# One list of instructions per engine in place of one list for TensorE and a greedy rule for the rest, with new planner constants

## The chip, the cores and the metric

The kernel runs on one core of one Trainium2 chip. The core has five engines that each work through their own stream of instructions in order and meet at semaphores: TensorE (PE, matrix products), VectorE (DVE), ScalarE (ACT, function tables), GpSimd (POOL) and SyncE (SP, which here issues nearly all DMAs). The metric is device time in microseconds for one execution. The median of three runs before the change is 3925.85 us (3921.62 to 3927.92).

## What is computed

The reference is a small vision tower: patches to tokens, one attention layer whose keys go through a Fourier series, and a mixture-of-experts network. There are 16 images of 3 x 512 x 512, which give 1024 tokens of width 256 each. Cut to what matters:

```
h = patches(x) @ W.T + b                      # 1024 tokens, 768 -> 256, per image
z = layernorm(h);  q, k, v = split(z @ w_qkv) # 8 heads of 32
k = sum_f a_f * sin(f*k) + b_f * cos(f*k)     # f = 1..256, elementwise
h = h + softmax(q k^T / sqrt(32)) v @ w_out + b_out
z = layernorm(h)
shared = relu(relu(z@sW1+sb1)@sW2+sb2)@sW3+sb3
experts = 4 networks 256 -> 128 -> 64 -> 256
h = h + shared + sum over the 2 best experts of softmax weight * expert
```

## The kernel before, in words

All times lie in `plain_path`; a second path, `general_path`, is only entered when a verdict computed on the chip asks for it.

The work on one image falls into two kinds. The first is a fixed repeating stream:

- The keys of a pair of heads are turned into angles (`keys`), written to DRAM and read back spread over partitions. `load_waves` (SP, two DMAs per tile) brings two tiles `w` per group; `load_source` and `spread_waves` (DVE shuffle) make a third, `f`. `turn_waves` (POOL) multiplies each with a lane number, `sine` (ACT) takes the sine. One group is thus three POOL and three ACT instructions.
- `mix` (M, PE, in 64x32 tiles of the array) forms partial sums of the series, `times_fast` (DVE) multiplies them, `add_up` (R, PE, 128x32 tiles) adds two groups up. 32 groups make one image, 8 groups one pair of heads. Then `finish_keys` (DVE) rounds the pair's keys and writes them to DRAM, and `stack_keys` (SP) reads them back, stacked, into the one buffer `k4`, for which the last score of the pair before must be done.
- `score` (S, PE, whole array), `exponential` (ACT, the Exp table) and `weigh` (W, PE, 128x32 tiles) are the attention: 8 key blocks for each of 8 (pair, half) attentions of an image; `normalize` (DVE) divides.

S and M write to the same pool `big` of two PSUM buffers, so the third taker has to wait until the first has been read (by the exponential, or by the product). ScalarE needs a table load (`ACT_TABLE_LOAD`) whenever it goes from sines to exponentials or back. `load_waves(g)` may only overwrite the tile that `mix(g - 4)` has read. SP issues in order, so a load that waits for its mix holds back what is queued behind it.

The second kind is everything else: tokens, layer norms, queries, values, projection, gates and networks. It is written as Python generators in four chains, 0 to 3; each `yield` names the engine of the next step. Steps of the kind "either" run with the whole array or as four 128x32 tiles, whichever tiling TensorE already has (`tiling_of`).

Nothing is scheduled at run time. While the program is built, a planner keeps a clock for each engine and places instructions one after the other; the streams that come out are fixed. In the kernel before, TensorE's order is a written string, `ORDER` (M, R, S, W or the number of a chain, 3840 tokens, of which 240 repeat 11 times). `lay_fixed` (L437) and `run` (L452) place its tokens. For SP, POOL, ACT and DVE, `others` (L408) takes whatever can start first by the planner's clock. Each step has a cost in the planner (the number in `yield ACT, 0.6` or `put(ACT, "fixed", 0.99, ...)`), and there are global constants: `LAG` between engines, `LANDS` for a DMA's landing, `SWITCH` for a change of tiling, `TABLE` for a table load.

Of the kernel before, what the change touches and what calls it, by code (L numbers as in the profile page):

```python
# [23 lines left out]
NT = N // P  # L24
# [33 lines left out]
LAG, LANDS, TABLE, PER_COLUMN = 0.06, 2.0, 1.28, 1.0 / 600  # L58
SWITCH = {None: 0.21, (128, 32): 0.13, (64, 32): 0.13}

TILINGS = {"mix": (64, 32), "av": (128, 32), "red": (128, 32)}
USERS = {"M": "prod", "S": "exp"}
KINDS = {"M": "mix", "R": "red", "S": "score", "W": "av"}
COLUMNS = (128, 32)
ORDER = (
    "333333313133100003000030M0M000MMR3R3M3M",
    "303RMM3MR330M3R3M03MSSRSSWSSWSSWWWW0MWM",
    "WMMRSSSRSWSSWSSW0WWWWMMW3MMRSSRSSWSSWSSW0WW0MMWWWMMRSSRSSWSSWSSW0WWMWWMWMRMSSSWSSWSSWSRW"
    "WWWWMMMMRSSSWSSWSSWSRWWWWW0M0MM0RMS0SSWSSWSWSWSWWW3W3MR13M3MMRSSRSSWSS1SSWWWW3WMWWM3RMS1"
    "SS1SS0SSWWWMS3WR3WWWWM0MMRMS0SS1SR1SSWW1S1SW0W1WW1MMW1W1MM1SSRWSS0SS1WSSWW10RWMWWW1MM10M"  # L70
    "S1SSRWSWR1SS1WSS1W1MMWWMMWW0SS1R1SS1WW1SS1SSW1WRW1WMMW3WMMRS1SS1SW1SS3SSW1WR1WWWWWMM13MM"
    "1RSS0SS0SS0SWWWSWWWR3MMW1WS10S1RSS1S3MMWSS3WRWWSW1WWMW31MM0SS1SSRMS1SSWWWSWR3WWWW3MM131M"
    "S1RSSWWMWSSR3S1S3S1WWW01M1WW1MM0RSS1SWSSWMS1SSWRWW01MW1WWMM101SSRMW1SSWWSS1RSS101MMWWWWW"
    "MS3SSWRMWSS1S01SSW1RW0W3MMWWRWSS131SS1MMWWSS1SSRWWW1WWW101",
    (
        "MM10RMM1SS01SS1SS1WWSS1WWWRWWWMM10MMRS3S1SS1SSWWWSS3RWWWW1W3MM0RMM3SSRSWWWSS1SS1S3WWWMMW"
        "3W311MSRM1WS1S3SWWS3S1SSRW1W0WMM1WWRMM10SS1SS1WW1SS0SSWWRW1WWW0MM10MM1SS1RRWWSS0S1SWSS1W"
        "WWWWMM1S0SRWSSWMMWS1S31SSWRW3WW1WMM3MMR1SS1SS1SSWWWSS1WRWW1WW101"
    )
    * 11,  # L80
    "MM1MM1SSRRWWS1S0SS0SSWWW130MMWW1WRM1MS1",
    "3SSRWWWSS31SS1SW1WWWWMM3RM1S0SSWSS1SSWWMSWR3WWM3WWMM13S1SR1MSWWRS3S1SWS3SWWW01MM1WW10MMR"
    "1SS1SSRWSS1S1WWS0WWWWWMM101MM1SS1RS1SRSSWWWSS01WWMMWWWMS1SSWSSRW0SS1S1WMWWR1WWMM10W1MMR1"
    "SS1SSWWSS1SSWWWR1WM1WW101MM10S1MR1SSWRS1SWSSWS1WWMMWWWRMM1SS0SSWWSSWSSRWWW1WW1M0M1RSS1SS"
    "WSSWSMWSM1WWRWM1W1WMM1RM1SS1SSWWSS1SSWR1W1W1W1MM1WWR1SM1SS1SSWWSSWS1MWWRWMWWM1SS1SWSMSRM"
    "WS1SS1WR1WWW1WW1MM1M1RSS1SWWSS1SSWSWMWW1RW1MM1RW1MM1SSR1SSWWSS1WWSSWWWW1SSSWSSWWSSWSSWWW"
    "W1SS1SS1SWWSSWWWWWW11110110111110000101000100101001000100",
)

@with_exitstack  # L90
def plain_path(ctx: ExitStack, tc: tile.TileContext, a: dict, out: bass.AP, verdict: bass.AP):
# [179 lines left out]
    def retile(tiling):  # L271

        same = now["tiling"] == tiling
        now["tiling"] = tiling
        return 0.0 if same else SWITCH[tiling]

# [53 lines left out]
    def step(c):  # L330
# [9 lines left out]
        if on:  # L340
            at = max(clock[on], ch["ready"] + LAG)
            if on == PE:
                at = max(at, banks(c)[0][0] + LAG)
            ch["ready"] = clock[on] = at + (need[1] or 0.0)
            if bank is not None:
                free[bank] = ch["ready"]
        elif isinstance(need, tuple):
            ch["ready"] = max(ch["ready"], done[need])
# [11 lines left out]
        if on == PE:  # L360
            took = PER_COLUMN * (now["stream"] - before) + retile(now["piece"])
            now["piece"] = None
            ch["ready"] = clock[PE] = at + took
# [16 lines left out]
    def wanting(engine):  # L380

        for c, ch in enumerate(chains):
            need = ch["need"]
            if ch["gen"] is None or callable(need) or need[0] != engine:
                continue
            if engine == ACT and len(need) > 2 and now["table"] != need[2]:
                continue
            at = max(clock[engine], ch["ready"] + LAG)
            if engine == PE:
                if not banks(c):  # L390
                    continue
                at = max(at, banks(c)[0][0] + LAG)
            yield at, c

    def lay(engine, queue):
        cost, deps, key, action = queues[engine][queue].pop(0)
        at = begin(engine, deps)
        clock[engine] = at + cost
        done[key] = clock[engine]
        action()  # L400

    def heads(engine):
        for rank, (name, steps) in enumerate(queues[engine].items()):
            at = begin(engine, steps[0][1]) if steps else None
            if at is not None:
                yield at, rank, name

    def others(limit):  # L408

        soonest = None  # L410
        again = True
        while again:
            again = False
            soonest = None
            for engine in (SP, POOL, ACT, DVE):
                while True:
                    settle()
                    best = min(heads(engine), default=None)
                    chain = min(wanting(engine), default=None)
                    if chain and (  # L420
                        best is None
                        or chain[0] < best[0]
                        or (chain[0] == best[0] and best[2] not in ("prod", "keys"))
                    ):
                        at, lay_it = chain[0], lambda c=chain[1]: step(c)
                    elif best:
                        at, lay_it = best[0], lambda q=best[2]: lay(engine, q)
                    else:
                        break
                    if at > limit:  # L430
                        soonest = at if soonest is None else min(at, soonest)
                        break
                    lay_it()
                    again = True
        return soonest

    def lay_fixed(kind):  # L437

        cost, deps, key, action = queues[PE][kind][0]
        user = USERS.get(kind)  # L440
        at = begin(PE, deps + (bigs[-2:-1] if user else []))

        def lay_it():
            queues[PE][kind].pop(0)
            clock[PE] = done[key] = at + cost + retile(TILINGS.get(KINDS[kind]))
            if user:
                bigs.append((user, *key[1:]))
            action()

        return at, lay_it  # L450

    def run():  # L452

        order = "".join(ORDER)
        for i, token in enumerate(order):
            now["ahead"] = order[i + 1 : i + 4]
            while True:
                soonest = others(clock[PE])
                if token in KINDS:
                    at, lay_it = lay_fixed(token)  # L460
                else:
                    c = int(token)
                    at = next((at for at, one in wanting(PE) if one == c), None)
                    lay_it = lambda: step(c)
                if at is not None and (soonest is None or at <= max(soonest, clock[PE])):
                    break
                assert soonest is not None
                others(soonest)
            lay_it()
        while (soonest := others(clock[PE])) is not None:  # L470
            others(soonest)
        assert not any(q for e in queues.values() for q in e.values())
        assert not any(ch["gen"] for ch in chains)
# [4 lines left out]
    def load_x(b, j):  # L478

        b, j = b + j // (N // XT), j % (N // XT)  # L480
        if b < B:
# [5 lines left out]
            done["x", b, j] = transfer(1.75, 0.6, clock[PE])  # L487
# [38 lines left out]
    def tokens(b, half):  # L526
# [5 lines left out]
        for t in range(4):  # L532
# [14 lines left out]
            yield DVE, 0.41  # L547
# [95 lines left out]
    def values(b):  # L643
# [5 lines left out]
        for t0 in range(0, NT, 2):  # L649
# [11 lines left out]
            yield ACT, 0.62  # L661
# [142 lines left out]
    def networks(b, half, late=False):  # L804
# [25 lines left out]
        def first_of_expert(e):  # L830
            yield ANY
            ps = hidden(lambda c: w1e[:, 2 * e + c, :], "e1p")
            yield ACT, 0.6
# [4 lines left out]
        def second_of_experts(u, e1):  # L838
# [11 lines left out]
            yield ACT, 0.6  # L850
# [15 lines left out]
        for m in range(2):  # L866
            yield ANY
            ps = hidden(lambda c, m=m: w1s[:, c, ts(m, P)], "s1p")
            yield ACT, 0.6
# [14 lines left out]
        yield ACT, 0.6  # L884
# [57 lines left out]
    def load_waves(g, j):  # L942
# [13 lines left out]
        put(SP, "waves", 1.1, deps, ("load", g, j), action)  # L956
# [29 lines left out]
    def spread_waves(g):  # L986
# [11 lines left out]
        put(DVE, "spread", 1.28, deps, ("spread", g), action)  # L998

    def turn_waves(g, j):  # L1000
# [8 lines left out]
        put(POOL, "turn", 1.87, [dep], ("turn", g, j), action)  # L1009

    def sine(g, j, change):
        def action():
            now["table"] = AF.Sin
# [6 lines left out]
        put(ACT, "fixed", 0.96 + change, [("turn", g, j)], ("sine", g, j), action)  # L1020
# [26 lines left out]
    def times_fast(g):  # L1047
# [4 lines left out]
        put(DVE, "prod", 1.16, [("mix", g), ("sine", g, 2)], ("prod", g), action)  # L1052
# [76 lines left out]
    def score(att, kc):  # L1129
# [13 lines left out]
        put(PE, "S", 0.47, deps, ("score", att, kc), action)  # L1143

    def exponential(att, kc):
        def action():
            now["table"] = AF.Exp
# [7 lines left out]
        put(ACT, "fixed", 0.99, deps, ("exp", att, kc), action)  # L1155
# [28 lines left out]
    def normalize(att):  # L1184
# [8 lines left out]
        def divide(half):  # L1193
# [11 lines left out]
            put(DVE, "norm", 0.4, deps, ("divide", att, half), action)  # L1205
# [15 lines left out]
        put(DVE, "norm", 1.67, [("av", att, NT - 1)], ("reciprocal", att), reciprocal)  # L1221
        for half in range(2):
            divide(half)
        put(DVE, "norm", 0.4, [("divide", att, 1)], ("norm", att), check)
# [45 lines left out]
    for rd in range(B * RI + 2):  # L1270
# [3 lines left out]
        for g in groups[::2]:  # L1274
            first = g == groups[0]
            for i, j in ((0, 0), (0, 1), (1, 0), (1, 1), (0, 2), (1, 2)):
                sine(g + i, j, TABLE if first and i == j == 0 else 0.0)
# [761 lines left out]
```

## Time and profile before

| | us |
|---|---|
| median of the runs | 3925.85 |
| the profiled execution, its own time | 3924.07 |
| its span, first to last instruction | 3922.5 |
| TensorE busy in the span | 3810.0 (97%) |
| ScalarE busy | 3263.0 (83%) |
| GpSimd busy | 3193.6 (81%) |
| VectorE busy | 2531.7 (65%) |
| mean granted TensorE clock | 0.994 |

The time of the profiled execution is the span and 1.6 us around it. Lines are read as: line of the kernel, engine, operation, tile written and tiles read, number of instructions, then busy time, mean duration and the idle time of the engine just before them with what ended it. Ends of matrix products are modelled in the profile and they overlap, so a TensorE that is shown as busy may be waiting inside a record: the distance between the ends of successive products tells more than the busy time. The sixteen images follow one another every 235 to 239 us in the middle of the run.

### The profile page before, as it was taken

To read this page: it belongs to the slowest core of one execution; us is meant where nothing else is said; L and a number is where in the kernel's file an instruction comes from. 1 tells how busy PE (TensorE), PEld (TensorE's weight loads), DVE (VectorE), ACT (ScalarE), POOL (GpSimd) and SP (SyncE) were. 2 spreads that over 40 slices of the span, in tenths; PEclk is the share of its full clock that TensorE was granted. 3 is DMA by queue.
4 is the path that set the end of the run, shared out by engine and by line. 5 is a ranking of instruction groups with operands and counts; after the bars stand their busy time and mean duration, and the time that the engine had idled before them with its cause. 6 is when DMAs were issued, how large, how long until landed. Compare 5 with 4: busy or idle time off the path is not lost.

```text
span 3922.5 us, 102737 instructions
## 1 busy us (share of the span) xinstructions
PE 3810.0 (97%) x40337; PEld 1948.9 (50%) x40337; DVE 2531.7 (65%) x4075; ACT 3263.0 (83%) x3939; POOL 3193.6 (81%) x2328
## 2 busy tenths in 40 slices
PE   7899999999999999999999999999999999999998
PEld 4334454554545555455454545545455454544444
DVE  4656757667675766757667675776767767576652
ACT  2788888888888888888888888888888888888983
POOL 3998878788788878879788788878879888888860
PEclk9999999999999999999999999999999999999999
DMA  7987968888787888979889788798878889788860
GB/s 228 281 261 217 278 192 245 259 226 258 220 257 225 237 264 224 259 216 256 235 233 265 212 257 247 224 265 224 262 218 255 247 229 265 216 245 235 221 170 18
DMA packets 587615, 916.51 MB, mean 234 GB/s; under 512 B 58828, under 2 KB 177524, under 8 KB 587124
## 3 DMA queue, kind: packets, MB, share of 16 engines
q1 hardware_dynamic: 580880, 906.98, 80.6%
q8 instruction: 321, 5.26, 0.6%
q10 hardware_dynamic: 6244, 2.88, 0.3%
q14 instruction: 170, 1.39, 0.1%
HBM read 758.64 MB, written 150.99 MB: 232 GB/s over the span
## 4 chain that ended last, share of the span: by engine, by line
PE 66%; DMA 13%; ACT 8%; POOL 5%; DVE 4%; issue 3%; SPq 2%; ACTq 0%; POOLq 0%; DVEq 0%
PE av L1167 17%; PE sT L1134 10%; PE kan L1036 8%; DMA w<-ud 7%; PE red L1069 4%; PE e1p L301 3%; PE tok L301 3%; ACT w L1016 3%; POOL w L1006 3%; PE e3p L301 2%; PE tok L304 2%; DMA k<-kd 2%; PE s1p L301 2%; PE e1p L304 2%; ACT f L1016 2%
## 5 line engine op out<-in xcount | busy, mean ns | idle before, releaser
L1006 POOL TENSOR_TENSOR w<-w,lane 128x1024 int32<-128x1024 int32 x1024 | 1923.6, 1895 | 406.9 <-DMA w<-ud 275.7
L1149 ACT ACTIVATE es<-sT 128x1024 f32<-128x1024 f32 x1024 | 1014.3, 1022 | 357.3 <-PE sT L1134 312.2
L1016 ACT ACTIVATE w<-w 128x1024 f32<-128x1024 int32 x1024 | 1013.4, 1046 | 67.5 <-POOL w L1006 64.3
L1006 POOL TENSOR_TENSOR f<-f,lane 128x1024 int32<-128x1024 int32 x512 | 970.2, 1895 | 102.0 <-DVE f L991 84.8
L1134 PE MATMUL sT<-q,k 128*128 128x512 f32 x2048 | 707.6, 454 | 42.9 <-DMA k<-kd 13.4
L1050 DVE TENSOR_TENSOR f<-kan,f 128x1024 f32<-128x1024 f32 x512 | 605.2, 1214 | 203.1 <-ACT f L1016 116.3
L991 DVE STREAM_SHUFFLE f<-src 128x1024 int32<-128x1024 int32 x512 | 681.3, 1370 | 0.4
L1167 PE MATMUL av<-es,v 128*32 128x256 f32 x8192 | 638.8, 383 | 3.5 <-DVE rc L1208 2.6
L1167 PE MATMUL av<-es,ones 128*32 128x256 f32 x8192 | 630.9, 379 | 0.0
L1036 PE MATMUL kan<-w,coef 64*32 64x512 f32 x8192 | 540.1, 598 | 18.8 <-ACT w L1016 12.6
L1016 ACT ACTIVATE f<-f 128x1024 f32<-128x1024 int32 x512 | 519.0, 1046 | 4.1 <-POOL f L1006 4.1
L1134 PEld LDWEIGHTS sT<-q,k 128*128 128x128 f32 x2048 | 351.2, 190 | 340.0 <-issue 146.0
L1167 PEld LDWEIGHTS av<-es,v 128*32 128x32 f32 x8192 | 235.5, 109 | 343.2 <-issue 236.9
L1167 PEld LDWEIGHTS av<-es,ones 128*32 128x32 f32 x8192 | 267.2, 110 | 176.4 <-issue 1.4
L1191 DVE RECIPROCAL rc<-av 128x256 f32<-128x256 f32 x128 | 224.8, 1756 | 169.5 <-PE av L1167 169.5
L1036 PEld LDWEIGHTS kan<-w,coef 64*32 64x32 f32 x8192 | 129.1, 105 | 313.9 <-issue 133.4
L1069 PE MATMUL red<-f,pack 128*32 128x512 f32 x2048 | 271.0, 602 | 0.0
L301 PE MATMUL tok<-wt,x 128*128 128x256 f32 x768 | 182.1, 389 | 22.1 <-DMA w1s<-in_sW 12.5
L1016 ACT ACT_TABLE_LOAD x128 | 164.2, 1283 | 17.7 <-DMA w<-ud 15.5
L304 PE MATMUL tok<-wt,x 128*32 128x256 f32 x3072 | 178.0, 380 | 0.6 <-DVE h L548 0.6
L301 PEld LDWEIGHTS tok<-wt,x 128*128 128x128 f32 x768 | 147.4, 194 | 57.9 <-DMA w1s<-in_sW 12.4
L513 ACT ACTIVATE hn<-h,less,rstd 128x256 f32<-128x256 f32 x256 | 140.7, 591 | 39.8 <-POOL less L505 39.0
(148 smaller groups left out, 4269.5 us busy)
## 6 DMA issues: line engine op xcount, KB each, us to landing
w<-ud SPq DMA_DIRECT2D x2048, 256.0 KB
q<-qd SPq DMA_DIRECT2D x512, 128.0 KB
k<-kd SPq DMA_DIRECT2D x128, 512.0 KB
x<-in_xT SPq DMA_DIRECT2D x128, 384.0 KB
ud<-u SPq DMA_DIRECT2D x64, 512.0 KB
ud<-ui SPq DMA_DIRECT2D x64, 512.0 KB
src<-ud SPq DMA_DIRECT2D x512, 64.0 KB
qd<-qhi SPq DMA_DIRECT2D x64, 256.0 KB
```

The lines of the kernel that those rows point to most:

```text
L301: nc.tensor.matmul(out=out, lhsT=lhsT, rhs=rhs, start=start, stop=stop)
L304: nc.tensor.matmul(out=out[ts(i, 32)], lhsT=lhsT[:, ts(i, 32)], rhs=rhs, start=start, stop=stop)
L991: nc.vector.stream_shuffle(w, sources[g // 8].rearrange("p r n -> p (r n)"), [4 * (g % 8) + i // 8 for i in range(32)],)
L1006: nc.gpsimd.tensor_tensor(w, w, f.to_broadcast([P, N]), ALU.mult)
L1016: nc.scalar.activation(x, w, AF.Sin, scale=TURN * 2.0**-32)
L1036: nc.tensor.matmul(out=ps[ds(64 * j + 32 * blk, 32), ts(r, 512)], lhsT=coef[ts(r, 64)].rearrange("p e f j -> p (e f j)"), rhs=w[ts(r, 64), ...
L1050: nc.vector.tensor_mul(w, kan.pop(g), w)
L1069: nc.tensor.matmul(out=rows_of_pair[p][ts(2 * i + r, 32), :], lhsT=pack[:, ds(PACK0 - 16 * (k % 2) - 2 * (k // 2), 32)], rhs=prod[:, ts(r, ...
L1134: nc.tensor.matmul(out=ps[:, ts(s, 512)], lhsT=k4[:, 2 * s + kc // 4, ts(kc % 4, P)], rhs=q4[:, s, :], start=True, stop=True,)
L1149: nc.scalar.activation(es, scores.pop(kc), AF.Exp, scale=SCALE)
L1167: nc.tensor.matmul(out=acc[0][ts(i, HD), ts(half, 256)], lhsT=ones32 if half else v[:, kc, p % NPAIR, ts(i % 2, HD)], rhs=es[:, ds(512 * ( ...
L1191: nc.vector.reciprocal(rc[0], acc[0][:, 256:512])
```

## The change

The written order of TensorE is replaced by five lists, `ORDERS`, one for each engine, each in the planner's tokens (s, e, t for sine, exponential and table step on ACT; u, p, k, n, d for DVE's queues; o for POOL; c, w, k, q for SP's; digits are the chains). TensorE's list has 3840 tokens again, of which 240 now repeat 9 times. `others`, `heads` and `wanting` go; `head` looks at the first token of each engine's list, and `run` places the token that can start first:

```diff
-    def run():
-        order = "".join(ORDER)
-        for i, token in enumerate(order):
-            now["ahead"] = order[i + 1 : i + 4]
-            while True:
-                soonest = others(clock[PE])
...
+    def run():
+        settle()
+        while any(orders.values()):
+            ready = {e: h for e in orders if (h := head(e))}
+            engine = min(ready, key=lambda e: ready[e][0])
+            token = orders[engine].pop(0)
+            now["ahead"] = orders[PE][:3]
+            ready[engine][1]()
+            settle()
...
+    def head(engine):
+        if not orders[engine]:
+            return None
+        token = orders[engine][0]
+        if token.isdigit():
+            at = wanted(engine, int(token))
+            return at is not None and (at, lambda: step(int(token)))
+        queue = token if engine == PE else TOKENS[engine][token]
+        cost, deps, key, action = queues[engine][queue][0]
+        if engine == PE:
+            at = begin(PE, deps + (bigs[-2:-1] if user_of(token, key) else []))
+            return at is not None and (at, lambda: lay_fixed(token, at))
+        at = begin(engine, deps)
+        return at is not None and (at, lambda: lay(engine, queue, at))
```

The constants of the planner change as well, and it now charges a table load wherever the kind of function changes, and a tail after each instruction before another engine may use the result:

```diff
-LAG, LANDS, TABLE, PER_COLUMN = 0.06, 2.0, 1.28, 1.0 / 600
-SWITCH = {None: 0.21, (128, 32): 0.13, (64, 32): 0.13}
+LAG, LANDS, TABLE, PER_COLUMN, STALL = 0.07, 2.3, 1.29, 1.0 / 600, 0.15
+TAIL = {"pe": 0.27, "act": 0.08, "dve": 0.06, "pool": 0.0, "sp": 0.0}
+SWITCH = {None: 0.15, (128, 32): 0.12, (64, 32): 0.12}
...
-        put(SP, "waves", 1.1, deps, ("load", g, j), action)
+        put(SP, "waves", 1.38, deps, ("load", g, j), action)
...
-        put(POOL, "turn", 1.87, [dep], ("turn", g, j), action)
+        put(POOL, "turn", 1.853, [dep], ("turn", g, j), action)
...
-        put(ACT, "fixed", 0.96 + change, [("turn", g, j)], ("sine", g, j), action)
+        put(ACT, "sine", 0.946, [("turn", g, j)], ("sine", g, j), action)
...
-        put(ACT, "fixed", 0.99, deps, ("exp", att, kc), action)
+        put(ACT, "exp", 0.91, deps, ("exp", att, kc), action)
```

No operand, tile, pool or dependency of an instruction is changed, and the matrix products, vector operations and DMAs are the same in kind and number, apart from "either" steps that now run in another tiling and apart from table loads. The letter u and the branch for "sum" in `user_of` are never reached: no queue of that name is filled.

## The prediction

> **What bounds the kernel now.** I read the page first, then busy times by stretch, then TensorE's records one by one.
>
> ```profile
> PE 3810.0 (97%) x40337; PEld 1948.9 (50%) x40337; DVE 2531.7 (65%) x4075; ACT 3263.0 (83%) x3939; POOL 3193.6 (81%) x2328
> ```
> ```profile
> 0.00:80.00 80.00, 52.90 (x186) 36.34 (x187) 33.32 (x69) 11.17 (x16) 21.34 (x40) 0.94 0.70 219
> 80.00:280.00 200.00, 177.00 (x1824) 69.70 (x1824) 123.96 (x182) 160.39 (x180) 186.16 (x110) 0.97 0.93 271
> 280.00:985.00 705.00, 689.88 (x7563) 347.32 (x7562) 470.10 (x745) 604.23 (x727) 593.91 (x420) 1.00 0.83 239
> 985.00:3349.00 2364.00, 2340.79 (x25196) 1223.92 (x25188) 1580.14 (x2542) 2035.49 (x2461) 1994.14 (x1440) 1.00 0.85 241
> 3349.00:3800.00 451.00, 442.82 (x4829) 212.72 (x4825) 289.61 (x456) 401.45 (x487) 386.71 (x285) 1.00 0.80 226
> 3800.00:3923.00 123.00, 106.65 (x763) 58.87 (x753) 34.53 (x85) 50.28 (x72) 11.38 (x36) 0.95 0.11 32
> ```
>
> The columns are the stretch, its length, then busy time (and records) of PE, weight loads, DVE, ACT and POOL, the granted clock, DMA's share and GB/s. TensorE bounds the run; only from 80 to 280 us does POOL (186 of 200 us) set the pace. But "busy" hides two things, which the timeline shows:
>
> ```profile
> 1502.68 0.40 PE L301 MATMUL wb<-w,sel 128*128 128x512 f32 x1
> 1503.01 0.64 PE L1167 MATMUL av<-es,v 128*32 128x256 f32 x8
> ...
> 1510.49 1.06 PE L1036 MATMUL kan<-w,coef 64*32 64x512 f32 x12
> 1511.49 0.70 PE L301 MATMUL e3p<-w3s,s 128*128 128x256 f32 x2
> ...
> 1514.42 1.89 PE L301 MATMUL v<-wv,hnT 128*128 128x256 f32 x8
> 1516.24 1.09 PE L1036 MATMUL kan<-w,coef 64*32 64x512 f32 x16
> ```
>
> Each line is start, duration, shapes. In one tiling, a 256-column step ends 0.216 us after the one before, a 512-column step 0.429 (0.234 for scores), a transpose 0.109. When the tiling changes, the first end comes later: v ends at 1516.31, the second of two kan steps at 1517.33, so the first at 1516.90, 0.59 after v in place of 0.429. In the same way the first e3p ends 0.42 after the last kan, and the first av 0.35 after wb, both in place of 0.216. The medians over the trace are 0.161 into 64*32, 0.138 into 128*32 and 0.194 to 0.197 into 128*128. The second hidden thing is waiting for a free PSUM buffer or for data:
>
> ```profile
> 1296.54 0.73 PE L1134 MATMUL sT<-q,k 128*128 128x512 f32 x2 [0.67 <-ACT es L1149]
> ```
>
> So I split the time up to TensorE's last end, 3914.3 us: streaming 3517.7, 1260 changes of tiling 205.7, waits 190.9. By stretch the waits are 35.7 (0 to 80), 46.6 (80 to 279), 29.5 (279 to 985), 43.8 (985 to 3112) and 35.2 (the rest). Streaming can't change, since an "either" step takes the same in both tilings. The change can act on the last two terms alone.
>
> **Part 1: tilings, dearer.** Counting the changes in both programs' TensorE order, 1259 become 1406 (the trace has one more, at the verdict): 85 to 95 in the first image, 250 to 306 in the next three, 639 to 648 in the nine images that repeat (71 and 72 an image), 285 to 357 in the last three. Priced by kind: +1.6, +9.4, +2.3, +12.2. The first 1.6 lies where POOL sets the pace, so I cost it at nothing; without that cover it would be 1.6. Sum **+23.9**.
>
> **Part 2: waits for the two `big` buffers.** For each score or mix I took TensorE's own work between the end of the taker two places earlier and its start; that work must cover one exponential or product. In the trace, pairs under 0.9 us waited 2.76 (mix) or 0.58 (score), 0.9 to 1.2 waited 0.51, 1.5 to 1.8 waited 0.11 (score), 1.8 to 2.2 waited 0.22 (mix) or 0.01. Pairs under 1.8 fall from 147 to 86, in a repeating image from 5 to 1; under 1.2 from 28 to 6. Priced, outside the first image: 29.4 to 13.5, **-15.9** (bounds: none of it, -29.4). What is late next there is the exponential itself, behind more table loads.
>
> **Part 3: the start.** With POOL busy 186 of 200 us, at most 14 can go; I take **-4** (0 to -14), as the 36 first turns follow the same chain.
>
> **Part 4: a key load behind a waiting load.** In every repeating image the list of SP puts, for one pair of four, the load of a `w` tile that waits for a mix directly ahead of `k<-kd`. That mix ends 10.0 us of TensorE work before the first score of the pair; before the change it ended 32.4 before. The nearest case in the trace is the pair at 3592 us, with 10.8 us:
>
> ```profile
> 3599.65 2.67 SPq L951 DMA_DIRECT2D w<-ud  x4
> 3602.42 1.20 SPq L1098 DMA_DIRECT2D k<-kd  x2
> ```
> ```profile
> 3611.73 0.70 PE L1134 MATMUL sT<-q,k 128*128 128x512 f32 x2 [1.41 <-DMA k<-kd]
> ```
>
> From the issue of `k<-kd` to the score it took 9.3 us (8.1 to 10.1 where other pairs waited). With 0.3 us to the semaphore, 1.3 for one `w` load's two DMAs and 9.2 to land, 10.8 stand against 10.0: 0.9 us, bounds 0 and 1.8. Behind this load on SP wait the key load and all later loads; the score waits for it. Nine times: **+8** (0 to +16). Another pair of four, which waits 1.1 to 2.7 us now with 13.4 us between its last and first score, has the same 13.4 afterwards: no change.
>
> **Part 5: the other waits.** From 279 us on, 108.5 less the 29.4 of part 2 leave 79: sines and keys that come late, chain steps, and the dependent tail (15 of it after 3776 us). No row prices the new lists here. The bounds are -60 (a quarter left) and +10 (new waits in place of these, at the rate of part 4). I take half, **-40**, because the nearest thing I could count, part 2, falls by 54%, and because the new costs are the trace's own: a sine follows a sine after 0.947 us (planner 0.946, before 0.96), an exponential after 0.920 (0.91, before 0.99), a turn after 1.853 (1.853, before 1.87).
>
> **Part 6: table loads.** ACT's order holds 72 more, 328 for 256: 16 an image become 18 in the repeating ones, and 20, 22, 30, 20 at the start and 28, 26, 20 at the end.
>
> ```profile
> L1016 ACT ACT_TABLE_LOAD x128 | 164.2, 1283 | 17.7 <-DMA w<-ud 15.5
> L1284 ACT ACT_TABLE_LOAD x128 | 164.2, 1283 | 2.2
> ```
>
> From the load to the next start is 1.294 us, and an exponential ahead of a load takes 1.041 in place of 0.920, so one costs 1.41 and 72 cost 102 us of ACT. I cost them at nothing on the path: ACT is busy 3263 of 3922 us, and its largest waits are for TensorE:
>
> ```profile
> ACT es L1149 <- PE sT L1134: 312.2, 293, 7.6
> ACT es L1149 <- PE av L1167: 43.2, 70, 4.2
> ```
>
> If that cover is gone, up to 102 us appear; this is rival A. The Trainium skill ("ScalarE: Activation LUTs", section "What ACT_TABLE_LOAD costs") speaks against such a trade: 1.283 us for the load and about 1.38 us of drain, 2.66 a switch, by which 72 would be 191 us. The load agrees with the row, the drain does not: the trace shows 0.12 us of it.
>
> **Sum.** +23.9 - 15.9 - 4 + 8 - 40 = -28. Against the profiled execution's own 3924.07 that is 3896; the median of the runs lies 1.8 above it, so 3897 (rounded down from 3897.9).
>
> **Rivals.**
>
> A, slower: ACT becomes the bound where the loads pile up. The third image gets 14 more, 20 us, where ACT is busy 209.1 of 250 us now and waits for scores only 19.3; the fourteenth and fifteenth get 12 and 10. For it: a load ahead of an exponential delays the buffer that the next score needs by 1.41 us, as long as the exponential itself. Against: outside these places ACT idles 14%. It decides from 27% of the 102 us on, where the 28 us of the forecast are used up; with half of them, 3897 + 51 = 3948.
>
> B, no change: the waits of part 5 only move, and shrink by 12 in place of 40: 3897 + 28 = 3925. For it: the chain that ended last spends 13% in DMAs and 4% on DVE, which no list shortens. Against: part 2 is a count in the order itself, and it halves.
>
> C, more: part 5 gives 65 and part 4 nothing: 3897 - 25 - 8 = 3864. For it: 14 us of part 5's waits would still be there, which is what the dependent tail alone takes now. Against: DMA is 0.83 to 0.93 busy, so landings scatter, which no fixed list removes.
>
> **How the numbers follow.** A run tells about 0.2% (8 us) from no change: 3918 to 3934 counts as the same. Forecast 0.54, own range 3875 to 3918; C 0.11; B 0.14; A 0.21. B's share is nearly all "the same", and a little of the forecast's upper edge is too. Faster 0.65, same 0.14, slower 0.21. Best bounds: -14 + 23.9 - 29.4 - 60 = -79.5; worst without A: 0 + 25.5 + 16 + 10 = +51. Cutting a tenth on either side gives 3862 to 3944, which leaves out the best bounds and the worse half of A.
>
> **What would show it.** Right: waits between 985 and 3112 us fall below 35 in place of 43.8, images there come every 234 to 236 us, score waits on ACT under 1.8 us of cover are gone, ACT busy rises by about 92. Part 4 right: a score of one pair of four waits about 1 us for `k<-kd`. Wrong: ACT shows over 92% in the third image while scores wait for `es`; or waits at both ends stay at 30 and 35 while 21.6 us of extra tilings are paid there.

## The result, and the profile after

| | before | after |
|---|---|---|
| median of the runs compared, us | 3924.09 | 3945.80 |
| lowest and highest | 3921.62 to 3927.92 | 3937.77 to 3957.16 |
| the profiled execution's own time | 3924.07 | 3937.77 |
| ScalarE busy | 3263.0 | 3354.9 |
| table loads on ScalarE | 256 | 328 |

The change makes the kernel slower by 0.54%: the ratio is 1.0054, 95% interval 1.0032 to 1.0076. In a later comparison the same changed kernel took 3934.80 (11 runs, 3928.82 to 3957.64) beside 3923.19 for the one before (3915.41 to 3932.38), ratio 1.0043 (1.0027 to 1.0060). The sign is the same twice; the size is 11.6 us by the medians of one comparison and 21.7 by those of the other. The changed kernel scatters over 29 us there, the one before over 17.

The first line of the page after hardly differs from that of before. TensorE is still the busiest engine, at the same share; only ScalarE's number has moved, by 92 us:

```profile
PE 3816.6 (97%) x41069; PEld 1921.2 (49%) x41069; DVE 2521.7 (64%) x4075; ACT 3354.9 (85%) x4011; POOL 3193.0 (81%) x2328
```

Busy times by stretch of the changed kernel (stretch, length, busy time and records of PE, weight loads, DVE, ACT and POOL, granted clock, DMA's share, GB/s):

```profile
0.00:80.00 80.00, 50.81 (x185) 34.60 (x185) 32.13 (x69) 11.27 (x17) 21.38 (x40) 0.94 0.68 210
80.00:280.00 200.00, 175.35 (x1896) 68.21 (x1904) 120.20 (x175) 162.30 (x182) 185.80 (x110) 0.93 0.91 267
280.00:985.00 705.00, 692.12 (x7451) 340.22 (x7439) 473.22 (x747) 633.52 (x747) 591.19 (x419) 1.00 0.84 239
985.00:3349.00 2364.00, 2334.69 (x25948) 1204.55 (x25940) 1567.09 (x2537) 2071.29 (x2488) 1992.20 (x1440) 1.00 0.85 241
```

POOL sets the pace from 80 to 280 us as it did (185.80 against 186.16 of 200 us). Nothing here tells why the run is longer, since TensorE's busy time holds both changes of tiling and waits inside records. The sum over the distances between TensorE's ends tells it. It is made as in the prediction, up to TensorE's last end, for the profiled execution and for a second one of the same kernel (3930.38 us):

| us | before | after | after, second |
|---|---|---|---|
| streaming | 3517.7 | 3517.0 | 3517.0 |
| changes of tiling | 205.7 (1260) | 231.2 (1407) | 231.2 (1407) |
| waits | 190.9 | 179.5 | 172.5 |
| of these: to 80 us | 35.7 | 32.5 | 34.6 |
| first image | 46.6 | 50.7 | 51.0 |
| images two to four | 29.5 | 23.0 | 23.7 |
| nine images that repeat | 43.8 | 42.6 | 30.2 |
| last three | 35.2 | 30.8 | 33.1 |

The tilings cost 25.5 us more and the waits give back 11.4 or 18.4. That is +13.4 or +6.4 with the 0.7 of streaming, against +13.7 and +6.3 between the executions' own times. Both profiled executions took less than their kernel's median (3937.77 beside 3945.80, 3930.38 beside 3934.80), so a typical execution loses some 4 to 8 us more than the sum shows. Its instructions are the same, so that these are more waits is likely, but no profile shows it. All else of the document is about these two numbers: whether the 25.5 are really paid, and why the waits gave so little.

Where the waits of the repeating images lie has changed. Waits of mixes fell from 12.2 to 1.5 us. First scores of a pair of heads, which need the keys just read back, wait longer: their waits rose from 14.3 us (all in the third pair of four) to 30.3 (7.9 in the first pair of four, 22.4 in the third); 24.2 in the second execution. The sync queue shows the place that the prediction named, ahead of the first pair of four at 1540 us. The load of a `w` tile stands ahead of `k<-kd`, 3.3 us after the write of the keys was issued:

```profile
1540.36 0.35 SPq L1200 DMA_DIRECT2D kd<-khi  x1
1541.09 0.90 SPq L1200 DMA_DIRECT2D kd<-klo  x1
1544.35 1.16 SPq L1064 DMA_DIRECT2D w<-ud  x2
1545.62 1.20 SPq L1210 DMA_DIRECT2D k<-kd  x2
1546.91 4.24 SPq L1064 DMA_DIRECT2D w<-ud  x6
```

TensorE's timeline shows the score at the end of it, 9.5 us after the issue, with its wait in brackets:

```profile
1552.73 1.67 PE L438 MATMUL tok<-wt,x 128*128 128x256 f32 x7
1555.12 1.17 PE L1246 MATMUL sT<-q,k 128*128 128x512 f32 x4 [0.71 <-DVE h L661]
```

The engine named there, DVE, is not what the score reads; it needs `k` and `q` and a free buffer. The experiments below move `k<-kd` alone, and this wait goes with it.

### The profile page after: what moved, and what is told of

It is laid out like the page before. It is cut to its first block, busy times and chain, and to the rows that moved or that the text cites. A ratio compares the mean times of both kernels' runs of the same rounds, so it can differ in the third digit from the quotient of the medians.

```text
span 3936.2 us, 103969 instructions
## 1 busy us (share of the span) xinstructions
PE 3816.6 (97%) x41069; PEld 1921.2 (49%) x41069; DVE 2521.7 (64%) x4075; ACT 3354.9 (85%) x4011; POOL 3193.0 (81%) x2328
## 4 chain that ended last, share of the span: by engine, by line
PE 71%; DMA 11%; ACT 7%; DVE 4%; issue 3%; POOL 2%; SPq 2%; ACTq 0%; POOLq 0%; DVEq 0%
PE av L1278 18%; PE sT L1246 11%; PE kan L1148 9%; DMA w<-ud 6%; PE red L1181 5%; PE tok L441 4%; PE e3p L438 3%; ACT w L1128 3%; PE e1p L438 2%; PE tok L438 2%; PE e1p L441 2%; DMA k<-kd 2%; PE s1p L438 2%; PE proj L438 1%; ACT es L1260 1%
## 5 line engine op out<-in xcount | busy, mean ns | idle before, releaser
L1260 ACT ACTIVATE es<-sT 128x1024 f32<-128x1024 f32 x1024 | 1012.2, 1023 | 295.6 <-PE sT L1246 266.1
L1246 PE MATMUL sT<-q,k 128*128 128x512 f32 x2048 | 701.0, 452 | 46.9 <-DVE st L610 12.4
L1148 PE MATMUL kan<-w,coef 64*32 64x512 f32 x8192 | 529.1, 601 | 7.9 <-ACT w L1128 3.0
L1278 PEld LDWEIGHTS av<-es,ones 128*32 128x32 f32 x8192 | 266.4, 110 | 175.6
L1181 PE MATMUL red<-f,pack 128*32 128x512 f32 x2048 | 280.1, 613 | 3.2 <-DVE f L1162 3.1
L441 PE MATMUL tok<-wt,x 128*32 128x256 f32 x3744 | 216.5, 379 | 3.7 <-DVE h L661 3.7
L441 PEld LDWEIGHTS tok<-wt,x 128*32 128x32 f32 x3744 | 121.0, 110 | 89.3 <-DVE h L661 6.0
L438 PE MATMUL tok<-wt,x 128*128 128x256 f32 x600 | 140.4, 385 | 15.8 <-DMA w1s<-in_sW 12.5
L974 DVE TENSOR_TENSOR e<-wb,e 128x512 f32<-128x512 f32 x64 | 44.0, 688 | 171.6 <-PE wb L438 167.1
```

What stands on the lines that cost most here:

```text
L438: nc.tensor.matmul(out=out, lhsT=lhsT, rhs=rhs, start=start, stop=stop)
L441: nc.tensor.matmul(out=out[ts(i, 32)], lhsT=lhsT[:, ts(i, 32)], rhs=rhs, start=start, stop=stop)
L1148: nc.tensor.matmul(out=ps[ds(64 * j + 32 * blk, 32), ts(r, 512)], lhsT=coef[ts(r, 64)].rearrange("p e f j -> p (e f j)"), rhs=w[ts(r, 64), ...
L1181: nc.tensor.matmul(out=rows_of_pair[p][ts(2 * i + r, 32), :], lhsT=pack[:, ds(PACK0 - 16 * (k % 2) - 2 * (k // 2), 32)], rhs=prod[:, ts(r, ...
L1246: nc.tensor.matmul(out=ps[:, ts(s, 512)], lhsT=k4[:, 2 * s + kc // 4, ts(kc % 4, P)], rhs=q4[:, s, :], start=True, stop=True,)
L1260: nc.scalar.activation(es, scores.pop(kc), AF.Exp, scale=SCALE)
```

## The experiments

Two theories were open. One: waits for what DMAs land can't be saved by another order, and the extra tilings are paid in full ("landings"). The other: the 72 more table loads on ScalarE eat what the lists save ("table loads", rival A of the prediction). A third possibility was that SP's list alone is at fault.

**The key load ahead of the waiting load.** One list of SP, in the part that repeats nine times, one letter moved:

```diff
-            "wwwwwwwwkwwwwwwccwcwqwcwwqwwwwwwkwwwqwwwwcwwcccwwwwqwwkwwwwqwwwwccwcwcwwwqwwwkww"
+            "wwwwwwwwkwwwwwwccwcwqwcwwqwwwwwkwwwwqwwwwcwwcccwwwwqwwkwwwwqwwwwccwcwcwwwqwwwkww"
```

> The changed kernel with one letter moved in SP's repeating list: for one pair of heads of four, in nine images, the key reload stands ahead of the w load that waits for a late mix. Theory 1 (the waits that went from the buffers came back at the key reload on SP's queue): the 7.9 us that the first scores of these nine pairs wait shrink to 0 to 3, and the whole kernel gains 4 to 8 us against the changed kernel. Theory 2 (DMAs land late and unevenly whatever the order; a wait taken away shows up at the next place): the first scores wait as long, or the gain is under 3 us and other scores wait more.

Measured: 3968.45 us, ratio to before 1.0116 (1.0101 to 1.0131). The first scores of the first pair of four wait no more (7.9 and 6.8 us became 0.0), and yet the waits of the repeating images rose to 68.4, of which scores have 54.6. What is late next can be read on GpSimd and ScalarE. The unmoved list first, in the second execution of the changed kernel near 1550 us (POOL, then ACT):

```profile
1549.37 2.39 POOL L674 TENSOR_TENSOR h<-h,bout 128x1024 f32<-128x1024 f32 x1
1551.72 1.90 POOL L1120 TENSOR_TENSOR w<-w,lane 128x1024 int32<-128x1024 int32 x1
1557.81 1.90 POOL L1120 TENSOR_TENSOR w<-w,lane 128x1024 int32<-128x1024 int32 x1 [4.19 <-DMA w<-ud]
...
1553.65 1.06 ACT L1129 ACTIVATE w<-w 128x1024 f32<-128x1024 int32 x1
1554.72 1.28 ACT L1394 ACT_TABLE_LOAD   x1
```

and the same place with the letter moved:

```profile
1560.00 2.40 POOL L673 TENSOR_TENSOR h<-h,bout 128x1024 f32<-128x1024 f32 x1
1564.93 3.75 POOL L1119 TENSOR_TENSOR w<-w,lane 128x1024 int32<-128x1024 int32 x2 [2.53 <-DMA w<-ud]
...
1566.86 1.06 ACT L1128 ACTIVATE w<-w 128x1024 f32<-128x1024 int32 x1 [2.59 <-POOL w L1119]
1567.93 1.28 ACT L1393 ACT_TABLE_LOAD   x1
1569.34 3.77 ACT L1260 ACTIVATE es<-sT 128x1024 f32<-128x1024 f32 x4
```

In the unmoved list the turn after `h<-h,bout` runs at once, and POOL waits only before the next one. With `k` first, the `w` load is issued 8.2 us after the last score of the pair before in place of 7.4 (means of the nine), POOL waits before the first turn, the sine waits for that turn, and ScalarE's list has this sine ahead of the pair's exponentials. The keys were on time, and the exponentials were not. Scores then wait for the exponentials of the scores two before them; from 985 to 3349 us that group went from 0.3 and 0.6 us in the two executions of the unmoved list to this:

```profile
PE sT L1246 <- ACT es L1260: 20.9, 19, 2.9
```

Some 7 us saved at the keys thus cost 34 to 45 elsewhere in the same images, 26 to 38 on balance. The load that stands in the way of `k<-kd` is, by way of POOL and ScalarE, the more urgent of the two. Theory 1 of the expectation had the wait right and its price wrong; theory 2's "other scores wait more" is what happened.

**The same for the third pair of four as well.**

```diff
-            "wwwwwwwwkwwwwwwccwcwqwcwwqwwwwwwkwwwqwwwwcwwcccwwwwqwwkwwwwqwwwwccwcwcwwwqwwwkww"
+            "wwwwwwwwkwwwwwwccwcwqwcwwqwwwwwkwwwwqwwwwcwwcccwwwwqwwkwwwwqwwwwccwcwcwwwqwkwwww"
```

> As the one before, and for the pair two later the key reload also stands ahead of the two w loads (four DMAs) that are queued right in front of it; that pair's first scores wait 22.4 us in all in the nine images, 14.3 in the kernel before. Theory 1: 8 to 16 us faster than the changed kernel, the 22.4 falling to about 14 or less. Theory 2: no faster than the changed kernel by more than 3 us, because the w loads now land later and mixes wait for them (the 1.5 us that mixes wait in the middle rises to 8 or more).

Measured: 4027.31, ratio 1.0268 (1.0252 to 1.0283). The third pair's first scores wait 5.9 us in place of 17.4 to 22.4, and the waits of the repeating images grow to 127.7. The expectation looked for the new waits at the mixes, but these stay at 1.8 us; 79 of the 127.7 are waits of `av`, which needs the exponentials, and 47 of scores. The exponentials are late again, by more. The run also shows why the third pair waits longer than before the change. Its key load is issued no sooner here (4.4 us after the last score of the pair before, 4.6 in the changed kernel), but without four `w` DMAs issued ahead of it, it takes some 8.2 us from issue to the score where it took 9.8.

**SP without its list.** SP takes whichever load can start first by the planner's clock; the four other lists stay.

```diff
+GREEDY = (SP,)
...
+    def soonest(engine):
+        best = None
+        for queue, steps in queues[engine].items():
+            at = begin(engine, steps[0][1]) if steps else None
+            if at is not None and (best is None or at < best[0]):
+                best = at, lambda queue=queue, at=at: lay(engine, queue, at)
+        return best
...
+        if engine in GREEDY:
+            return soonest(engine)
```

> The changed kernel with the lists of PE, ACT, DVE and POOL, but SP's queue filled as before the change: whatever load can start first by the planner's clock. If SP's list is what keeps the gain away (theory 1), this is 5 to 20 us faster than the changed kernel, and its runs scatter less (the changed kernel's lie 20 us apart, the kernel before's 6). If not, it is within 5 us of the changed kernel and scatters the same.

Measured: 4040.51, ratio 1.0305 (1.0290 to 1.0320); waits 282.0. With the four other lists as they are, SP's list is worth over 90 us against the greedy rule, so going back to that rule on SP alone would not have helped. A better list for SP is not excluded by this.

**The changed kernel once more**, for a second set of times and a second profile:

> The changed kernel once more, unchanged, beside the others on one chip: 3938 to 3957 us, and the scatter of its runs, which the others are compared with. A profile of a slower run than the first, at 3937.77, would show which waits grow: by theory 1 those of the first scores of a pair, by theory 2 many places by a little.

Measured: the 3934.80, a little under what was expected, and the waits of the third column above. Between the two profiles the waits of the repeating images differ by 12.4 us for the same streams of instructions.

**Half of the `w` traffic.** From the ninth group on, one of the two loads of each `w` tile is left out, and the lane product reads a constant tile in its place. So this part of the series is not computed; the instructions on all engines and their order stay. Done to both kernels:

```diff
-            for c in range(2):
+            for c in range(2 if g < 8 else 1):
...
-            nc.gpsimd.tensor_tensor(w, w, f.to_broadcast([P, N]), ALU.mult)
+            src = quarter.to_broadcast([P, N]) if j < 2 and g >= 8 else w
+            nc.gpsimd.tensor_tensor(w, src, f.to_broadcast([P, N]), ALU.mult)
```

> The kernel before with half the traffic of its largest DMA stream: from the ninth group on each w tile gets one of its two loads, and the lane product takes its values from a constant in place of the tile, so the output is not the reference's. Same order otherwise. Landing theory (loads that land late and unevenly are what the lists could not plan away, and the wait goes on from POOL to ACT to TensorE): DMA's share falls from 0.85 to about 0.55 in the middle, first scores of a pair stop waiting, and 10 to 30 us go; the waits for the two big buffers (about 20 us) stay. Table theory (72 more table loads are what keeps ScalarE late): no more than 10 us go.

> The changed kernel with the same half of the traffic taken away (the output is not the reference's). Landing theory: it gains more than the kernel before does, 25 to 60 us, its waits in the middle nine images fall from 30 to 43 us to under 12, and it ends level with or up to 30 us ahead of the kernel before with half the traffic. Table theory: it stays 5 to 20 us behind that kernel, as now.

Measured: before 3890.25, ratio 0.9918 (0.9901 to 0.9934); after 3895.90, ratio 0.9935 (0.9918 to 0.9951). The stretch from 985 to 3349 us, first before, then after, shows DMA's share at 0.57 and 0.58 where it was 0.85:

```profile
985.00:3349.00 2364.00, 2348.44 (x25372) 1229.02 (x25370) 1596.27 (x2555) 2051.64 (x2479) 2008.77 (x1453) 1.00 0.57 171
```
```profile
985.00:3349.00 2364.00, 2354.06 (x26246) 1214.65 (x26238) 1573.53 (x2562) 2097.80 (x2523) 2015.11 (x1456) 1.00 0.58 172
```

The changed kernel gains 39 us from this (3934.80 to 3895.90; 42 by the ratios), the one before 34. Its waits in the repeating images fall from 42.6 or 30.2 to 16.1, of which first scores have 2.2; before's fall from 43.8 to 32.1. Its four runs scatter over 6 us where eleven scattered over 29. Here the lists save 20.0 us of waits, 138.0 in all against 158.0, where under the full traffic they save 11.4 or 18.4. The tilings cost 25.5, so even then the kernel before stays ahead, by 5.65 us (5.5 by the sum). The landing theory asked for waits under 12 in the repeating images and for a kernel level or ahead; neither came. First scores hardly wait in either kernel now, so their waits do end with landings. But to take half the traffic away adds only 1.6 or 8.6 us to what the lists save: landings explain a part of the loss, not the whole.

**No table loads in the loop.** The sines become a plain scaling, and the exponential's argument is made a thousandth, in both kernels: neither series nor softmax is computed, the instructions' durations stay.

```diff
-            nc.scalar.activation(x, w, AF.Sin, scale=TURN * 2.0**-32)
+            nc.scalar.activation(x, w, AF.Identity, scale=TURN * 2.0**-32)
...
-            nc.scalar.activation(es, scores.pop(kc), AF.Exp, scale=SCALE)
+            nc.scalar.activation(es, scores.pop(kc), AF.Exp, scale=SCALE * 1e-3)
```

> The kernel before with Identity in place of the sine (and a smaller scale in the exponential so that nothing overflows; the output is not the reference's): the same instructions, but no table load in the loop, so ScalarE has 256 x 1.41 = 361 us less to do. Landing theory: 0 to 25 us faster, since ScalarE mostly waited for scores. Table theory: 20 to 60 us faster.

> The changed kernel with the same done to it, 328 x 1.41 = 462 us less for ScalarE. Landing theory: it gains about what the kernel before gains, and stays 5 to 20 us behind it. Table theory: it gains 15 to 30 us more than the kernel before does and ends level or ahead.

Measured: before 3917.89, ratio 0.9984 (0.9974 to 0.9994); after 3923.13, ratio 1.0003 (0.9989 to 1.0017). ScalarE is now busy alike in both pages, first before, then after:

```profile
PE 3800.4 (97%) x40337; PEld 1946.9 (50%) x40337; DVE 2524.5 (64%) x4075; ACT 2931.7 (75%) x3683; POOL 3193.7 (82%) x2328
```
```profile
PE 3801.2 (97%) x41069; PEld 1919.9 (49%) x41069; DVE 2526.6 (64%) x4075; ACT 2925.9 (75%) x3683; POOL 3193.4 (81%) x2328
```

To lose 331 us of ScalarE's work is worth 6.3 us to the kernel before, and to lose 429 is worth 11.7 to the changed one by the medians (15.7 by the ratios). So the 72 extra loads, 98 us of ScalarE, cost some 5 to 9 us on the path, not 51. The intervals of the ratios are as wide as that (the changed kernel's without loads reaches from 0.9989 to 1.0017), so the 5 to 9 is a rough size. The place agrees with the prediction: in the changed kernel waits of images two to four fall from 23.0 and 23.7 to 18.9, those of the last three from 30.8 and 33.1 to 24.1, together by 11 to 14 us; in the kernel before the same two fall by about 8. Those of the repeating images, 40.2, lie between the two values with loads. And with no load in either, the changed kernel is still 5.2 us behind.

The Trainium skill prices a change of table at 2.66 us ("ScalarE: Activation LUTs", section "What ACT_TABLE_LOAD costs"). An estimate from that figure is 872 us of ScalarE for the changed kernel's 328. The runs show 429 us of ScalarE gone with them, 1.31 each, so the load itself agrees and the rest of the page's price is not seen here; the time moved by 12 to 16 us.

**The price of a tiling.** In the kernel before, every "either" step is run in the whole array. TensorE's tokens stay in order; the other engines are laid anew by the greedy rule.

```diff
-        if now["tiling"] in (None, COLUMNS):
-            return now["tiling"]
-        ahead = [t for t in now["ahead"] if t in "RSW"]
-        return COLUMNS if ahead and ahead[0] != "S" else None
+        return None
```

> The kernel before, with every step of the kind either run in the whole array, so that TensorE's order of tokens is the same but 1552 changes of tiling stand for 1260. By the prices of the trace that is 257.2 us in place of 205.7, +51.5, in a program that streams the same. Theory 'a change of tiling costs its price on the path, as TensorE has next to no slack': 3955 to 3980, with the waits at 175 to 205 us against 190.9. Rival 'the added changes are taken out of waits that would be there anyway': under 3940, with the waits down by 35 us or more.

Measured: 3980.88 beside 3925.93, +55.0, ratio 1.0135 (1.0114 to 1.0156). The sum shows 1553 changes for 257.3 us (+51.6), streaming 3517.5, and waits 196.9, six more than before. Here a change of tiling costs its price on the path, and nothing is taken out of the waits for it. The rival is out for the kernel before; in the changed kernel the price is read from the distances alone.

**The constants alone.** Costs, `LAG`, `LANDS`, `TABLE` and `SWITCH` of the change in the kernel before, with its written order and its greedy rule (the tails are left out, since the code before has no place for them):

```diff
-LAG, LANDS, TABLE, PER_COLUMN = 0.06, 2.0, 1.28, 1.0 / 600
-SWITCH = {None: 0.21, (128, 32): 0.13, (64, 32): 0.13}
+LAG, LANDS, TABLE, PER_COLUMN = 0.07, 2.3, 1.29, 1.0 / 600
+SWITCH = {None: 0.15, (128, 32): 0.12, (64, 32): 0.12}
...
-        put(SP, "waves", 1.1, deps, ("load", g, j), action)
+        put(SP, "waves", 1.38, deps, ("load", g, j), action)
```

> The kernel before, with its written order of TensorE and its greedy rule, and only the planner's constants of the changed kernel (LAG 0.07, LANDS 2.3, TABLE 1.29, SWITCH, and the costs of load, turn, sine, spread, product, score and exponential). TensorE's order and its 1260 changes of tiling stay; SP, POOL, ACT and DVE are ordered anew. Theory 'the gain of the change comes from the lists, and the constants alone bring little': within 8 us of before (3916 to 3932), waits in images 4 to 12 between 35 and 50 us against 43.8. Rival 'the truer durations alone save the waits, and the lists' extra 25 us of tilings spoil it': the 20 us of waits that the lists save appear here without the tilings, 3900 to 3912.

Measured: 3960.78, ratio 1.0097 (1.0081 to 1.0113). Both theories miss it: neither within 8 us nor a gain, but +35. The repeating images are untouched (waits 43.1 against 43.8); 26 of the 33 us of new waits lie in the first image. SP's queue there tells why, after the keys of the second pair were written:

```profile
194.53 0.38 SPq L1088 DMA_DIRECT2D kd<-klo  x1
...
203.45 2.46 SPq L951 DMA_DIRECT2D w<-ud  x4
208.32 0.39 SPq L483 DMA_DIRECT2D x<-in_xT  x1
208.80 7.58 SPq L951 DMA_DIRECT2D w<-ud  x12
216.50 1.41 SPq L1098 DMA_DIRECT2D k<-kd  x2
```

The key load is issued 22 us after the write, behind sixteen DMAs for `w`, and the score waits 16.8 us for it at 228 us. That the longer landings in the planner made the greedy rule put `k` so late is argued, not shown. What the run does show is that truer constants without the lists save nothing in the repeating images.

**The waiting score a step later, in both kernels.** In the part that repeats, a step of chain 0 goes ahead of the third pair's first score. Before (greedy rule for the other engines), and after (all other lists as they are):

```diff
-        "WWWWMM1S0SRWSSWMMWS1S31SSWRW3WW1WMM3MMR1SS1SS1SSWWWSS1WRWW1WW101"
+        "WWWWMM10SSRWSSWMMWS1S31SSWRW3WW1WMM3MMR1SS1SS1SSWWWSS1WRWW1WW101"
```
```diff
-            "R1RSS01SSWWWSS1WWWWWMM1SSR0WSSWMMWS1S3S1SRWWWW3MM1W3MM1RSS1SSWWSS1SSW1RWWW1WW101"
+            "R1RSS01SSWWWSS1WWWWWMM10SSRWSSWMMWS1S3S1SRWWWW3MM1W3MM1RSS1SSWWSS1SSW1RWWW1WW101"
```

> The kernel before, with one step of a chain (0, a query or network step) put ahead of the first score of the third pair of four instead of behind it, 11 times. That score's waits are 14.3 us over images 4 to 12, 1.6 us each. Theory 'a first score that waits for its keys gains when work that does not need them goes ahead': its waits fall to 0 to 7 us over these images, time 3910 to 3921. Rival 'the wait only moves to the exponentials and sines behind': first scores fall, the sum of waits stays at 186 to 196, time 3920 to 3928.

> The changed kernel with the same step of a chain put ahead of the first score of the third pair of four, two scores and one addition earlier, 9 times; all other lists kept. That score's waits were 22.4 us in one execution and 17.4 in another. Theory 'late keys': they fall below 10, time 5 to 12 us under the changed kernel's 3930 to 3946. Rival 'what the lists plan next is late instead': first scores fall, sum of waits stays at 170 to 182, time as the changed kernel's.

Measured: before 3948.13, ratio 1.0061 (1.0046 to 1.0076), slower; after 3936.72, ratio 1.0033 (1.0020 to 1.0047), as the changed kernel was. The first scores did what was asked: 14.3 to 2.3 us in the one, 22.4 or 17.4 to 8.8 in the other. The waits moved on, further than either theory had it for the kernel before. In the changed kernel the first pair's first scores went from 7.9 or 6.8 to 12.2, waits for the exponential in `av` to 10.5, and the sum to 175.6, between its two earlier values. In the kernel before the sum grew from 190.9 to 218.9; transposes of the layer norm, which waited 2.4 us in the repeating images, wait 23.9. The list of waits gives the chain backwards (total, times, longest). Before, from 985 to 3140 us:

```profile
ACT hn L513 <- POOL less L505: 18.5, 21, 2.5
...
POOL f L1006 <- DVE f L991: 35.4, 37, 3.2
```

and with the step moved:

```profile
PE lnT L310 <- ACT hn L513: 14.7, 26, 1.3
...
ACT hn L513 <- POOL less L505: 40.0, 29, 3.4
...
POOL f L1006 <- DVE f L991: 57.4, 43, 4.6
```

DVE's shuffles come later, POOL waits for them, ScalarE's norms wait for POOL, TensorE for the norms. The greedy rule laid DVE, POOL and ScalarE anew for this run, so it is the order of all engines that answers for the 22 us, not the step on TensorE by itself.

No version that beats both kernels came of this; the kernel before stays the fastest of those that compute the reference. TensorE's new list with the greedy rule for all the rest, which would show that list apart from the four others, wasn't tried, nor were more `w` buffers, which would let loads start earlier.

## Why the prediction was wrong, point by point

The forecast was 3897, faster, with 3875 to 3918 as its own range; the kernel became slower, and the median of 3945.80 lies 1.8 us above even the wide range of 3862 to 3944. The step that failed is part 5, which put -40 us on waits that hardly fell.

The traces tell the parts apart. Waits after the first image, by part 2's own measure (TensorE's work between the taker two places earlier and this one), are, to within 0.4 us of the sums above:

| us | before | after | after, second | before, half traffic | after, half traffic |
|---|---|---|---|---|---|
| part 2: takers with under 1.8 us of cover | 25.9 | 7.1 | 6.9 | 22.2 | 6.4 |
| part 4: first scores of the first pair, repeating images | 0.0 | 7.9 | 6.8 | 0.0 | 2.2 |
| part 5: the rest | 82.2 | 81.4 | 73.5 | 57.8 | 52.4 |
| sum | 108.1 | 96.4 | 87.2 | 80.0 | 61.0 |

- **Part 1 (+23.9)** was right. The changes of tiling cost 25.5 more in the trace after, the 1.6 in the first image among them, and the price stands up: 293 changes added on purpose cost 55 us where 51.6 was their sum.
- **Part 2 (-15.9)** was right in kind: waits of mixes in the repeating images fell from 12.2 to 1.5 us. It was right in size too: takers with under 1.8 us of cover wait 19 us less in the trace.
- **Part 3 (-4)** was wrong in sign. The first image ended 281.8 us after the start (284.2 in the second execution) in place of 278.6. POOL sets the pace as before, and its turns did not come earlier.
- **Part 4 (+8)** was right: 7.9 us, then 6.8, and 0.0 when `k` went first. But the sentence beside it, that the other pair of four has "no change", was wrong. The distance of 13.4 us between last and first score was the same, as counted; what had changed is what stands in the queue. In the changed kernel four `w` DMAs are issued between the write of the keys and `k<-kd`, none before the change, and the pair waited 22.4 or 17.4 where it had 14.3. These 8.1 or 3.1 us stand in the rest of the table.
- **Part 5 (-40)** is the step that failed. The rest of the waits went from 82.2 to 81.4 us, and to 73.5 in the second execution: -0.8 and -8.7 in place of -40. The half was carried over from part 2, a count of buffer pairs in TensorE's own order, to waits that are no such count. Late landings alone don't explain it. With half the traffic this rest is smaller in both kernels, and the lists still take only 5.4 us from it; without table loads, 4.9. Why the lists shorten the rest so little isn't shown by any run. The largest piece of it that can be named, the third pair's first scores (22.4 and 17.4 us, 14.3 before the change), is 0.0 in both kernels with half the traffic, so these scores wait for key loads that land late. With the parts as measured the sum comes out: 25.5 of tilings, -18.8, +0.9 up to 280 us, +7.9, -0.8 and -0.7 of streaming make +14.0, beside 13.7 between the executions' own times.
- **Part 6 (nothing)** was off by a little: the 72 loads cost 5 to 9 us, most of it, as far as the sums tell, in images two to four and at the end. The added 92 us of ScalarE were as forecast, and so was the cover: ScalarE's wait for scores shrank from 312.2 to 266.1 us.

```profile
ACT es L1260 <- PE sT L1246: 266.1, 293, 6.7
```

- **Rival A** gave 3948, close to the measured time by luck: it put half of 102 us on the path, and the loads cost 5 to 9. Without any load the changed kernel is still behind. **Rival B**, waits that only move, was the nearest: it let part 5 shrink by 12, and it shrank by 0.8 and 8.7. B's zero became +13.4 and +6.4 by this, by the 1.6 us of tilings in the first image, which weren't hidden, and by part 3, where waits up to 280 us rose by 0.9 and 3.3 in place of falling by 4; part 2's extra 3 us went the other way. The 5 to 9 us of the table loads lie mostly inside part 5.
- The signs asked for were half there. "Waits at both ends stay at 30 and 35 while 21.6 us of extra tilings are paid there" is nearly what happened: 23.0 and 30.8, with 21.6 paid. Below 35 between 985 and 3112 us was met in one execution (30.2) and not in the other (42.6).

## What to carry to other kernels

A price that is a count in the order (changes of tiling, pairs of buffers) could be trusted here, and the tilings were paid in full on an engine without slack; a saving in the other waits can't be carried over from such a count, and belongs near nothing until a run shows it. A load that waits at the head of an in-order queue may well stand in its best place: before moving something ahead of it, follow what the delayed load feeds, here GpSimd, the sine and then the exponentials, to the engine that bounds the run. And when a plan buys shorter waits with more of something dear, compare the two section by section: here 21.6 of the 25.5 us were spent at the ends, where waits fell by 7.9 to 10.9.

## What was not expected of the hardware

- The same streams of instructions scatter with the traffic: the changed kernel over 29 us (3928.82 to 3957.64, eleven runs) at a DMA share of 0.85, over 6 (3894.06 to 3900.03, four runs) at 0.58. Between two profiled executions the waits of the repeating images differed by 12.4 us. That the landings scatter is argued from this, not shown.
- The granted clock from 985 to 3349 us was 1.00 before and after, and lower where loads came late: 0.99 with one key load moved, 0.98 with two, 0.99 with SP's greedy list. From 80 to 280 us it was 0.97 before and 0.93 after (0.94 in the second execution). No run tells whether this is a cause of any time or follows from the waits.
